# Involution patches by 19 transposes at shifted rows instead of 7 transposes and DMA copies inside SBUF

## The chip, the cores and the metric

The kernel runs on one core of a Trainium2 chip. Its time is the device time of one execution in microseconds (us); the median of the runs is what counts. A profile shows one further execution. All data are f32.

The engines in the profile: PE (matrix products; PEld is its weight load), DVE and ACT (vector and scalar engine), POOL (GpSimd) and SP, which here only issues DMAs. PE's products land in PSUM, eight banks of 512 f32 for each of 128 partitions; the other engines carry them on from there.

## The reference

The input is `x` of 4 images, 256 channels, 56 x 56. Four layers follow each other, each of the form `x = x + layer(group_norm(x))`:

- layer 0, an involution: every pixel has its own 7 x 7 filter for each of 16 groups of 16 channels, made from the pixel's normed channels by two 1x1 convolutions (256 to 64, 64 to 49 x 16).
- layer 1, two 3x3 convolutions with batch norm, relu and a residual.
- layer 2, an involution again, with batch norms and relu.
- layer 3, a gate: the mean real part of a Fourier transform gives one factor per channel.

The involution, cut to what matters:

```python
kern = einsum('bchw,oc->bohw', h, span_w) + span_b        # 49 taps per group and pixel
kern = kern.reshape(b, G, 1, K * K, Ho, Wo)               # G = 16, K = 7
patches = patches.reshape(b, G, c // G, K * K, Ho, Wo)    # the 7x7 surroundings of each pixel
out = (kern * patches).sum(axis=3)
```

## The kernel before

Layers 0 and 2 share one function, `involution_layer`; layer 1 is `conv_layer` between them, and layer 3 is spread over layer 2. The change is in the involution.

An involution layer runs over 8 units: 4 images, 2 blocks `cb` of 128 channels (8 groups of 16). An image of 56 x 56 is cut into 7 columns (`tx`) of 8 pixels, and each column into 19 tiles (`ty`) of 3 x 8 pixels. The surroundings of a tile are 9 x 14 = 126 pixels (`Q`). So the involution of a tile is a matrix product over 126 pixels: a patch `xw` (126 pixels x channels) against a matrix `kt` (126 pixels x 24 outputs) for each group of channels.

A unit has two stages.

The tap stage (`tap_matrices`) makes `kt` of the whole unit: 32 groups of six products of the span table `z_sb` with the bottleneck's output `hp` (L596), each evicted with its bias by DVE (L615) or, every third, by ACT (L608). Callbacks (`hooks`) put other work between the groups.

The apply stage goes over the 7 columns. For each, `apply` multiplies the patches with `kt` (L637). An instruction computes several groups of channels against each other and only the diagonal blocks are wanted. `O_PARTS` (L50) sets two parts: tiles 0 to 9 with four groups at once (64 channels, 96 outputs), in two PSUM banks, and tiles 10 to 18 with two groups at once (32 channels, 48 outputs), in a third bank. ACT scales the first diagonal block into `un` (L650, L652), DVE adds the others (three, then one; L657), and POOL (layer 0, L662) or DVE (layer 2, L664) adds the result to the image.

The patches are made in `next_strip`, `begin_windows` and `next_windows`. `next_strip` norms a column with its borders into the single buffer `strip_sb`, 63 rows of 14 pixels (POOL, L390, or in layer 2 ACT, L388). `begin_windows` transposes 7 pieces of 9 rows on PE (L405): these are the patches of every third tile. `next_windows` copies them from PSUM into `xw` by ACT (L417). The other twelve patches are the same pixels three and six rows further down: four DMAs copy them inside SBUF from partition to partition (L423, L425), on SP's queue, in layer 0 one of them on POOL's. Three buffers `xw` (`NXW`) let the patches be made three columns ahead.

The main loop (L1026 to L1131) gives the order, and `in_order` holds every engine to the order of the program. After a unit's tap stage come the transposes for a column ahead (L1066), and after each column's `apply` the rest of `next_windows`, `next_strip` and the column's statistics (L1115). In layer 0, DVE and PE also prepare the next image (`sums`, `bottleneck`, whose products are L468 and whose evictions are L485 and L487). In layer 2, POOL gates the image before in chunks.

In layer 0, `z_sb` holds the table of all 16 groups. In layer 2 it holds 8, and `load_taps` (L581) loads the next unit's half from `z2_dram` during the apply stage (L1103). `tables2` writes `z2_dram` in layer 0's last units.

PSUM is handed out in pairs of banks (`two_banks`), four pairs in turn.

Of the kernel before, what the change touches and what calls it, by code (L numbers as in the profile page):

```python
# [10 lines left out]
F32 = mybir.dt.float32  # L11
# [38 lines left out]
O_PARTS = ((4, (0, 5), 5, 30), (2, (10,), 9, 26))  # L50
NXW = 3
# [20 lines left out]
def net_kernel(  # L72
# [45 lines left out]
    z2_dram = dram.tile([NB, P, GB, ZN], F32, name="z2_dram")  # L118
# [40 lines left out]
    def batch_norms():  # L159

        folds = (
            ("1", by_channel, L1_G1, L1_B1, L1_M1, L1_V1, NB),
            ("2", by_channel, L1_G2, L1_B2, L1_M2, L1_V2, NB),
            ("4", by_channel, L2_G, L2_B, L2_M, L2_V, NB),
            ("3", by_row, L2_G1, L2_B1, L2_M1, L2_V1, 1),
        )
        for name, par, _, _, _, var, n in folds:
            bn["s" + name] = const.tile([P, n], F32, name=f"bn{name}_s")
            bn["t" + name] = const.tile([P, n], F32, name=f"bn{name}_t")
            rsqrt_eps(bn["s" + name], par(var), BN_EPS)  # L170
        yield

        par_of = bn["par"] = {}
        for n in (2, 4):
            par_of[n] = const.tile([P, n], F32, name=f"par{n}_sb")
            nc.vector.tensor_reduce(
                par_of[n],
                ident_sb.rearrange("p (a e i) -> p e a i", e=n, i=GC),
                mybir.AxisListType.XY,
                ALU.add,  # L180
            )
            yield
        for i in range(3):
            for name, par, gamma, beta, mean, _, _ in folds:
                s, t = bn["s" + name], bn["t" + name]
                if i == 0:
                    nc.vector.tensor_mul(s, s, par(gamma))
                elif i == 1:
                    nc.vector.tensor_mul(t, par(mean), s)
                else:  # L190
                    nc.vector.tensor_sub(t, par(beta), t)
            yield

        s4 = bn["s4"]
        bn["s4"] = {}
        for n in (2, 4):
            bn["s4"][n] = const.tile([P, n, NB], F32, name=f"s4_{n}")
            for i in range(n):
                nc.vector.tensor_scalar_mul(bn["s4"][n][:, i, :], s4, par_of[n][:, i : i + 1])
            yield  # L200
# [98 lines left out]
    def involution_layer(layer, xin, xout, red, span, sb, xs_of, ahead=None, pending=None):  # L299

        with ExitStack() as es:
# [29 lines left out]
            z_sb = wpool.tile([P, G if layer == 0 else GB, ZN], F32, name="z_sb")  # L331
# [35 lines left out]
            strip_sb = wpool.tile([P, HS, QX], F32, name="strip_sb")  # L367
            if layer == 2:
                nc.gpsimd.memset(strip_sb, 0.0)

            def next_strip():
# [5 lines left out]
                st = strip_sb  # L377
# [14 lines left out]
            def window(ty):  # L392

                k, j = divmod(ty, TY)
                return (0, NSB, 2 * NSB - 1)[j] + k

            begun_windows = []

            def begin_windows():

                flat = strips[len(xws)].rearrange("p h w -> p (h w)")
                ps = two_banks().rearrange("p i n -> p (i n)")
                begun_windows.append(ps)
                for k in range(NSB):
                    nc.tensor.transpose(ps[:Q, k * P : (k + 1) * P], flat[:, k * Q : (k + 1) * Q], ident_sb)  # L405

            def next_windows():

                if len(xws) == len(columns):
                    return  # L410
                if not begun_windows:
                    begin_windows()
                ps = begun_windows.pop()
                xw = work.tile([Q, NTY, P], F32, name="xw", bufs=NXW)
                xws.append(xw)

                nc.scalar.copy(xw[:, :NSB, :], ps[:Q, : NSB * P].rearrange("q (n c) -> q n c", n=NSB))  # L417

                n = NSB - 1
                for j in range(1, TY):  # L420
                    cut = TY * QX * j
                    at = window(j)
                    nc.sync.dma_start(xw[: Q - cut, at : at + n, :], xw[cut:Q, 0:n, :])  # L423
                    eng = nc.sync if layer == 2 or j == 1 else nc.gpsimd
                    eng.dma_start(xw[Q - cut : Q, at : at + n, :], xw[:cut, 1 : 1 + n, :])  # L425

# [68 lines left out]
            def begin():  # L495
# [10 lines left out]
                nc.gpsimd.memset(strip_sb, 0.0)  # L506
# [74 lines left out]
            def load_taps(cb):  # L581

                nc.sync.dma_start(z_sb, z2_dram[cb])

            def tap_matrices(b, cb, hooks):
# [3 lines left out]
                for n in range(GB * TP // PB):  # L589
                    g, pb = divmod(n, TP // PB)  # L590
                    ps = two_banks()
                    for k in range(PR):
                        for i in range(2):
# [4 lines left out]
                                z_sb[i * R : (i + 1) * R, cb * GB + g if layer == 0 else g, z0 : z0 + Q],  # L598
# [26 lines left out]
            def apply(b, cb, kt, tx, xw):  # L625

                img = xs_of[b, cb].rearrange("p (h w) -> p h w", w=W)
                y0 = 0
                for ng, tys, nty, rows in O_PARTS:
                    pair = two_banks()  # L630
                    nb, m = len(tys), ng * GC
                    v = pair[:, :nb, : ng * nty * TP].rearrange("p i (e n) -> p i e n", e=ng)
                    for i in range(nb):
                        for k in range(nty):
                            ty = tys[i] + k
                            for j in range(P // m):
                                nc.tensor.matmul(  # L637
                                    v[m * j : m * j + m, i, :, k * TP : (k + 1) * TP],
                                    xw[:, window(ty), m * j : m * j + m],
                                    kt[:, ng * j : ng * j + ng, :, ty * NTX + tx, :],  # L640
                                    start=True,
                                    stop=True,
                                )
                    n = rows // nb * TX
                    o = [v[:, :, e, :n] for e in range(ng)]
                    un = work.tile([P, 2, O_PARTS[0][3] // 2 * TX], F32, name="un")
                    un = un.rearrange("p i n -> p (i n)")[:, : rows * TX]
                    part = un.rearrange("p (i n) -> p i n", i=nb)
                    if layer == 0:
                        nc.scalar.mul(part, o[0], bn["par"][ng][:, 0:1])  # L650
                    else:
                        nc.scalar.activation(  # L652
                            part, o[0], AF.Identity, bias=bn["t4"][:, cb : cb + 1], scale=bn["s4"][ng][:, 0, cb : cb + 1]
                        )
                    for e in range(1, ng):
                        s = bn["par"][ng][:, e : e + 1] if layer == 0 else bn["s4"][ng][:, e, cb : cb + 1]
                        nc.vector.scalar_tensor_tensor(part, o[e], s, part, ALU.mult, ALU.add)  # L657
                    dst = img[:, y0 : y0 + rows, tx * TX : (tx + 1) * TX]
                    y0 += rows
                    u = un.rearrange("p (r x) -> p r x", x=TX)  # L660
                    if layer == 0:
                        nc.gpsimd.tensor_tensor(dst, u, dst, ALU.add)  # L662
                    else:
                        nc.vector.scalar_tensor_tensor(dst, u, 0.0, dst, ALU.max, ALU.add)  # L664
# [166 lines left out]
            def last_normed(b, cb):  # L831
# [6 lines left out]
                else:  # L838
                    z = z_sb.rearrange("p g z -> p (g z)")
                    pieces = [z[:, k * n : (k + 1) * n] for k in range(2)]  # L840
                    pieces += [strip_sb.rearrange("p h w -> p (h w)")[:, :n], dead(b, cb, n, n)]
# [129 lines left out]
            else:  # L971
                since = mark()
                load_taps(0)
                nc.sync.dma_start(zb_sb, zb2_dram)
                next_strip()
                run(bottleneck(0))
                hooks0[3] = list(pending[0])
                for _ in range(NXW - 1):
                    next_windows()
                    next_strip()  # L980
                hooks0[7] = [next_windows, next_strip]
            if layer == 0:
                next_strip()
                for i in range(NXW):
                    hooks0.setdefault(2 + 5 * i, []).extend((next_windows, next_strip))
# [20 lines left out]
            def tables2():  # L1006
# [10 lines left out]
                for i in range(2):  # L1017
                    by = z2[i * R : (i + 1) * R].rearrange("r (cb g) z -> r cb g z", cb=NB)
                    for h in range(2):
                        to = z2_dram[:, h * R : (h + 1) * R].rearrange("cb r (g i) z -> r cb g i z", i=2)  # L1020
                        for c in range(NB):
                            nc.sync.dma_start(to[:, c, :, i], by[:, c])
# [3 lines left out]
            for u, (b, cb) in enumerate(units):  # L1026
# [39 lines left out]
                begin_windows()  # L1066
# [35 lines left out]
                if layer == 2 and u + 1 < len(units):  # L1102
                    late[1].append(lambda cb=cb: load_taps(1 - cb))  # L1103
# [13 lines left out]
                for tx in range(NTX):  # L1117
# [5 lines left out]
                    next_windows()  # L1123
                    next_strip()
# [644 lines left out]
```

## Time and profile before

| | us |
|---|---|
| runs (3), median | 1796.66 |
| runs, lowest to highest | 1794.62 to 1802.1 |
| the profiled execution | 1791.96 |
| its span, first to last instruction | 1790.2 |

The granted clock of PE was 0.983 on average. In that execution layer 0 runs to about 506 us, layer 1 to about 1238, and layer 2 to the end.

How to read the lines below. A line of groups has the source line, engine, operation, what is written and read, the shape (partitions x elements; for PE rows*columns of the weights first), the count, the busy time in us and the mean ns of one, and then the idle time of the engine just before and what ended it. "issue" is idle time in which the engine waited for nothing that the profile shows. PE's times overlap: matmuls are pipelined, and those in different parts of the array run at the same time, so a mean of 207 ns does not mean one in 207 ns. An f32 product is two matmul instructions, each with a weight load; an f32 transpose is one. Queue q8 brings PE's instructions.

### The profile page before, as it was taken

Reading aid. Unit: us, or ns where it says so; the run is one execution under the profiler, and the core shown is the slowest. Engines: PE = TensorE matmul, PEld = TensorE weight load, DVE = VectorE, ACT = ScalarE, POOL = GpSimd, SP = SyncE. Lnnn points to the kernel's source line nnn. Section 1 sums busy time; section 2 is a strip of 40 time slices with the busy share of each in tenths; the row PEclk is TensorE's granted clock in tenths of the full one; section 3 lists DMA queues with packets and bytes.
Section 4 is the critical chain, followed back from the end, with each engine's and each line's share of the span. In section 5 each row is a group of like instructions: output and inputs, shape, how many; then the busy total and the mean of one; then the engine's idle time right before and its main releaser. Section 6 shows DMA issues by size and latency. Waiting matters only on the chain.

```text
span 1790.2 us, 55795 instructions
## 1 busy us (share of the span) xinstructions
PE 1682.8 (94%) x24040; PEld 1469.8 (82%) x24040; DVE 1387.3 (77%) x2745; ACT 822.8 (46%) x1882; POOL 406.8 (23%) x627
## 2 busy tenths in 40 slices
PE   6999999999989999999999999999999899799887
PEld 4887888878878988898889888986887787688775
DVE  2777787776779988998899888985777687677675
ACT  2655556555642313231323122113768577577564
POOL 2224432344310000000000000001000464563572
PEclk9999999999989999999999999999999999999997
DMA  2445444644752112120112011122446667766753
GB/s 86 128 158 172 148 145 134 188 121 130 222 158 91 55 52 64 64 68 29 64 64 70 26 64 37 44 111 74 153 147 186 186 219 210 215 213 178 203 145 119
DMA packets 69043, 221.04 MB, mean 123 GB/s; under 512 B 13461, under 2 KB 23198, under 8 KB 65086
## 3 DMA queue, kind: packets, MB, share of 16 engines
q1 hardware_dynamic: 52302, 150.65, 27.1%
q0 software_dynamic: 14656, 64.77, 11.4%
q8 instruction: 190, 3.11, 0.7%
q10 hardware_dynamic: 1840, 2.05, 0.4%
q14 instruction: 55, 0.45, 0.1%
HBM read 80.91 MB, written 49.81 MB: 73 GB/s over the span
## 4 chain that ended last, share of the span: by engine, by line
PE 64%; DVE 20%; ACT 5%; issue 4%; DMA 4%; POOL 2%; SPq 1%; POOLq 0%; ACTq 0%; DVEq 0%
PE mm L1533 18%; PE ps L596 15%; PE ps L637 9%; PE mm L1451 9%; DVE kt L615 5%; PE mm L1422 5%; DVE un L657 4%; DMA xw<-xw 3%; PE ps L405 2%; PE ps L468 1%; ACT kt L608 1%; DVE st L1115 1%; DVE res L1526 1%; POOL strip_sb L390 1%; DVE xs L1385 1%
## 5 line engine op out<-in xcount | busy, mean ns | idle before, releaser
L596 PE MATMUL ps<-hp,z_sb 64*126 64x133 f32 x6144 | 387.6, 280 | 8.4 <-DVE kt L615 4.2
L637 PE MATMUL ps<-kt,xw 126*32 126x48 f32 (+1 forms) x12544 | 340.4, 223 | 53.3 <-issue 37.5
L596 PEld LDWEIGHTS ps<-hp,z_sb 64*126 64x126 f32 x6144 | 364.7, 186 | 27.7 <-DVE kt L615 6.2
L1533 PE MATMUL mm<-v,u_sb 128*128 128x280 f32 (+1 forms) x1728 | 383.5, 383 | 1.9 <-DVE u_sb L1264 1.5
L637 PEld LDWEIGHTS ps<-kt,xw 126*32 126x32 f32 (+1 forms) x12544 | 302.7, 118 | 99.4 <-issue 71.2
L615 DVE TENSOR_TENSOR kt<-ps,zb_sb 126x798 f32<-126x798 f32 x352 | 332.8, 980 | 63.8 <-PE ps L596 63.2
L1533 PEld LDWEIGHTS mm<-v,u_sb 128*128 128x128 f32 x1728 | 326.1, 189 | 56.3 <-DVE u_sb L1264 1.9
L608 ACT ACTIVATE kt<-ps,zb_sb 126x133 f32<-126x133 f32 x960 | 290.1, 492 | 101.0 <-PE ps L596 101.0
L1451 PE MATMUL mm<-v,u_sb 128*128 128x252 f32 (+1 forms) x936 | 209.7, 384 | 0.0
L1451 PEld LDWEIGHTS mm<-v,u_sb 128*128 128x128 f32 x936 | 176.5, 190 | 30.6 <-issue 0.8
L657 DVE SCALAR_TENSOR_TENSOR un<-ps,s,un 128x240 f32<-128x240 f32 x224 | 102.5, 458 | 90.6 <-ACT un L652 86.2
L1570 POOL DMA_DIRECT2D x<-xs x24 | 13.2, 549 | 680.1 <-DVE xs L1569 426.5
L657 DVE SCALAR_TENSOR_TENSOR un<-ps,par_sb,un 128x240 f32<-128x240 f32 x224 | 98.2, 456 | 77.7 <-ACT un L650 73.4
L1518 ACT ACTIVATE res<-xs,shift,norm_sb 128x1120 f32<-128x1120 f32 (+1 forms) x24 | 30.2, 1258 | 238.5 <-DVE xs L1569 107.3
L405 PE MATMUL ps<-ident_sb,strip_sb 128*126 128x128 f32 x784 | 113.2, 286 | 16.4 <-POOL strip_sb L390 10.5
L417 ACT COPY xw<-ps 126x896 f32<-126x896 f32 x112 | 101.4, 907 | 51.8 <-PE ps L405 43.3
L662 POOL TENSOR_TENSOR xs<-un,xs 128x240 f32<-128x240 f32 x112 | 72.3, 665 | 180.7 <-DVE un L657 180.5
L405 PEld LDWEIGHTS ps<-ident_sb,strip_sb 128*126 128x126 f32 x784 | 86.0, 143 | 28.0 <-POOL strip_sb L390 17.9
L652 ACT ACTIVATE un<-ps,bn_t,s 128x240 f32<-128x240 f32 x112 | 59.6, 538 | 101.4 <-PE ps L637 97.3
L1422 PE MATMUL mm<-xs,u_sb 128*128 128x126 f32 (+1 forms) x792 | 98.7, 277 | 2.1 <-DVE xs L1385 1.0
L650 ACT ACTIVATE un<-ps,par_sb 128x240 f32<-128x240 f32 x112 | 50.0, 448 | 104.0 <-PE ps L637 92.1
L1422 PEld LDWEIGHTS mm<-xs,u_sb 128*128 128x128 f32 x792 | 94.4, 191 | 3.5 <-DVE xs L1438 1.6
(256 smaller groups left out, 1905.8 us busy)
## 6 DMA issues: line engine op xcount, KB each, us to landing
xw<-xw SPq DMA_DIRECT2D x168, 252.0 KB
xw<-xw SPq DMA_DIRECT2D x224, 126.0 KB
xw<-xw POOLq DMA_DIRECT2D x56, 252.0 KB, 4.6
xs<-x SPq DMA_DIRECT2D x24, 560.0 KB
x<-xs POOLq DMA_DIRECT2D x8, 1568.0 KB
xs<-x SPq DMA_DIRECT2D x8, 1568.0 KB
xs<-in_x_dram SPq DMA_DIRECT2D x6, 1568.0 KB
x<-xs SPq DMA_DIRECT2D x6, 1568.0 KB
```

The lines of the kernel that those rows point to most:

```text
L405: nc.tensor.transpose(ps[:Q, k * P : (k + 1) * P], flat[:, k * Q : (k + 1) * Q], ident_sb)
L417: nc.scalar.copy(xw[:, :NSB, :], ps[:Q, : NSB * P].rearrange("q (n c) -> q n c", n=NSB))
L596: nc.tensor.matmul(ps[:Q, i, k * NT : (k + 1) * NT], z_sb[i * R : (i + 1) * R, cb * GB + g if layer == 0 else g, z0 : z0 + Q], hp[i * R : ...
L608: nc.scalar.activation(kt[:, g, pb, :, p], ps[:Q, i, k * NT : (k + 1) * NT], AF.Identity, bias=zb[:, p : p + 1],)
L615: nc.vector.tensor_tensor(kt[:, g, pb].rearrange("q t (i k) -> q t i k", i=2), ps[:Q, :, : PR * NT].rearrange("q i (k t) -> q t i k", k=PR ...
L637: nc.tensor.matmul(v[m * j : m * j + m, i, :, k * TP : (k + 1) * TP], xw[:, window(ty), m * j : m * j + m], kt[:, ng * j : ng * j + ng, :, ...
L652: nc.scalar.activation(part, o[0], AF.Identity, bias=bn["t4"][:, cb : cb + 1], scale=bn["s4"][ng][:, 0, cb : cb + 1])
L657: nc.vector.scalar_tensor_tensor(part, o[e], s, part, ALU.mult, ALU.add)
L662: nc.gpsimd.tensor_tensor(dst, u, dst, ALU.add)
L1422: nc.tensor.matmul(ps[:, co * m : (co + 1) * m], u[ci][:, co * P : (co + 1) * P], v2[:, e, : n // 2, ci * WT : (ci + 1) * WT], start=(ci = ...
L1451: nc.tensor.matmul(ps, u1_sb[:, ci, dy, k, co * P : (co + 1) * P], v[:, k, dy * NB + ci : (dy + n - 1) * NB + ci + 1 : NB, :], start=(j == 0),
L1533: nc.tensor.matmul(ps, u2_sb[:, ci, dy, k, co * P : (co + 1) * P], v[:, k, dy * NB + ci : (dy + n - 1) * NB + ci + 1 : NB, :], start=(j == 0),
```

## The change

The twelve patches that were copied are now transposed as well, each from its own rows of the strip: 19 transposes per column, in three groups of 7, 6 and 6. Each group has a pair of banks, and is copied to `xw` by ACT, ACT and DVE. No DMA copies remain.

All products are of two groups of channels (32 channels, 48 outputs). A column's 19 tiles lie in two banks of ten (tile 9 is computed in both), so that ACT scales, DVE combines and POOL or DVE adds once per column, 448 elements each.

There are two strips instead of one, two `xw` instead of three, one `un` instead of two. The patches are made one column less far ahead: `next_windows` is called whole, once after the tap stage and after each column but the last. The span table `z_sb` is kept whole in layer 2 too: one load at its start in place of one per unit.

```diff
-O_PARTS = ((4, (0, 5), 5, 30), (2, (10,), 9, 26))
-NXW = 3
+NG, NTB = 2, 10
+ROWS_B = H // 2
...
-            strip_sb = wpool.tile([P, HS, QX], F32, name="strip_sb")
+            strip_sbs = [wpool.tile([P, HS, QX], F32, name=f"strip_sb{i}") for i in range(2)]
...
-                xw = work.tile([Q, NTY, P], F32, name="xw", bufs=NXW)
+                flat = strips[len(xws)].rearrange("p h w -> p (h w)")
+                xw = work.tile([Q, NTY, P], F32, name="xw")
                 xws.append(xw)
-
-                nc.scalar.copy(xw[:, :NSB, :], ps[:Q, : NSB * P].rearrange("q (n c) -> q n c", n=NSB))
-
-                n = NSB - 1
-                for j in range(1, TY):
-                    cut = TY * QX * j
-                    at = window(j)
-                    nc.sync.dma_start(xw[: Q - cut, at : at + n, :], xw[cut:Q, 0:n, :])
-                    eng = nc.sync if layer == 2 or j == 1 else nc.gpsimd
-                    eng.dma_start(xw[Q - cut : Q, at : at + n, :], xw[:cut, 1 : 1 + n, :])
-
+                t0 = 0
+                for n, copy in ((7, nc.scalar.copy), (6, nc.scalar.copy), (6, nc.vector.tensor_copy)):
+                    ps = two_banks().rearrange("p i n -> p (i n)")
+                    for k in range(n):
+                        at = (t0 + k) * TY * QX
+                        nc.tensor.transpose(ps[:Q, k * P : (k + 1) * P], flat[:, at : at + Q], ident_sb)
+                    copy(xw[:, t0 : t0 + n, :], ps[:Q, : n * P].rearrange("q (n c) -> q n c", n=n))
+                    t0 += n
...
+                pair = two_banks()
+                v = pair[:, :, : NG * NTB * TP].rearrange("p i (e n) -> p i e n", e=NG)
+                m = NG * GC
+                for i in range(2):
+                    for k in range(NTB):
+                        ty = i * (NTB - 1) + k
+                        for j in range(P // m):
+                            nc.tensor.matmul(
+                                v[m * j : m * j + m, i, :, k * TP : (k + 1) * TP],
+                                xw[:, ty, m * j : m * j + m],
+                                kt[:, NG * j : NG * j + NG, :, ty * NTX + tx, :],
+                                start=True,
+                                stop=True,
+                            )
+                row = pair[:, 0, : ROWS_B * TX]
+                o = [
+                    bass.AP(row.tensor, row.offset + e * NTB * TP, [row.ap[0], [512 + TX, 2], [1, ROWS_B * TX]])
+                    for e in range(NG)
+                ]
+                un = work.tile([P, H * TX], F32, name="un", bufs=1)
...
-                begin_windows()
+                next_windows()
+                next_strip()
...
-                if layer == 2 and u + 1 < len(units):
-                    late[1].append(lambda cb=cb: load_taps(1 - cb))
...
                     apply(b, cb, kt, tx, xws[u * NTX + tx])
-                    next_windows()
-                    next_strip()
+                    if tx < NTX - 1:
+                        next_windows()
+                        next_strip()
```

## The prediction, made before the result

> **What bounds the kernel now.** I read the page first: who is busy, and which queues move what.
>
> ```profile
> PE 1682.8 (94%) x24040; PEld 1469.8 (82%) x24040; DVE 1387.3 (77%) x2745; ACT 822.8 (46%) x1882; POOL 406.8 (23%) x627
> ...
> q1 hardware_dynamic: 52302, 150.65, 27.1%
> q0 software_dynamic: 14656, 64.77, 11.4%
> q8 instruction: 190, 3.11, 0.7%
> ```
>
> PE sets the end, and the chain that ended last agrees (PE 64%, DVE 20%). So whatever PE is given or spared counts. Note the last line: PE's 24040 weight loads and 24040 matmuls arrive as 190 packets of 16 KB, one packet for some 126 pairs of a weight load and a matmul.
>
> The change lies in the "apply" stages: 7 columns of a unit, 16 units. Next, their groups with shapes kept apart:
>
> ```profile
> L637 PE MATMUL ps<-kt,xw 126*64 126x96 f32 x4480 | 228.9, 251 | 16.7 <-DMA xw<-xw 10.6 <-DVE un L657 3.5 <-issue 1.1
> L637 PE MATMUL ps<-kt,xw 126*32 126x48 f32 x8064 | 120.8, 207 | 36.6 <-issue 36.4
> L405 PE MATMUL ps<-ident_sb,strip_sb 128*126 128x128 f32 x784 | 113.2, 286 | 16.4 <-POOL strip_sb L390 10.5 <-issue 2.4 <-ACT hp L487 1.6
> L417 ACT COPY xw<-ps 126x896 f32<-126x896 f32 x112 | 101.4, 907 | 51.8 <-PE ps L405 43.3 <-DMA xw<-xw 8.1
> L657 DVE SCALAR_TENSOR_TENSOR un<-ps,s,un 128x240 f32<-128x240 f32 x168 | 78.5, 467 | 79.5 <-ACT un L652 75.2
> ```
>
> Divided by 112 columns: 40 matmul instructions of the 64-channel form, 72 of the 32-channel form (an f32 product is two), 7 transposes. The DMA copies that the change removes cost PE 10.6 us in all; "issue" cost it 36.4, nearly all in the 32-channel form. What "issue" is, the timeline of PE's weight loads shows (start, length, group, and in brackets the idle time before it):
>
> ```profile
> 321.83 2.39 PEld L637 LDWEIGHTS ps<-kt,xw 126*64 126x64 f32 x81 [0.17 <-issue]
> 325.00 0.41 PEld L637 LDWEIGHTS ps<-kt,xw 126*32 126x32 f32 x31 [0.78 <-issue]
> 325.47 0.75 PEld L405 LDWEIGHTS ps<-ident_sb,strip_sb 128*126 128x126 f32 x7
> 326.39 2.47 PEld L637 LDWEIGHTS ps<-kt,xw 126*64 126x64 f32 x88 [0.17 <-issue]
> 329.49 0.33 PEld L637 LDWEIGHTS ps<-kt,xw 126*32 126x32 f32 x24 [0.63 <-issue]
> 329.88 0.75 PEld L405 LDWEIGHTS ps<-ident_sb,strip_sb 128*126 128x126 f32 x7
> 330.80 2.53 PEld L637 LDWEIGHTS ps<-kt,xw 126*64 126x64 f32 x95 [0.17 <-issue]
> 334.19 0.27 PEld L637 LDWEIGHTS ps<-kt,xw 126*32 126x32 f32 x17 [0.86 <-issue]
> ```
>
> Between two stalls lie 31+7+88 = 126 and 24+7+95 = 126 pairs: exactly one packet of q8. PE runs out of instructions at the packet's edge, and 4.49 and 4.70 us pass from one resumption to the next, where the pairs alone stream in 3.7. In the trace's packet times a stalled PE resumes 1.2 to 1.65 us after the end of the newest q8 packet, and the next one starts only after PE has entered the block before it: one block is fetched ahead, no more. Call the time from entering a block to having the next one F.
>
> Last, three apply stages as windows (length, then busy time of each engine, clock, DMA share, GB/s):
>
> ```profile
> 190.50:217.20 26.70, 24.75 (x819) 21.97 (x819) 17.09 (x39) 11.18 (x19) 16.33 (x24) 1.00 0.53 152
> 245.20:279.60 34.40, 31.20 (x856) 25.30 (x855) 23.50 (x56) 17.48 (x39) 17.29 (x26) 1.00 0.47 131
> 1529.60:1565.10 35.50, 26.35 (x820) 22.71 (x819) 21.16 (x49) 17.66 (x25) 23.18 (x33) 1.00 0.81 223
> ```
>
> PE is busy through layer 0's stages (the second one also holds the next image's 56 long L468 matmuls); layer 2's wait more, under a DMA share of 0.8. In these three no other engine is over 70% busy.
>
> **The change, part by part.** Per column, on PE:
>
> Products: 112 instructions become 160 (2 x 10 x 4 products), all 32-channel. In unstalled runs 40 of the 64-channel form take 1.80 us to the next group and 72 of the other 0.91 (starts 11.0 ns apart). After: 160 x 11.0 ns + 0.13 = 1.89 us, where 2.71 was spent: -0.8.
>
> Transposes: 7 become 19. Seven take 0.91 us (0.109 to 0.118 apart, and the switch); 19 take 2.2 to 2.4: +1.4. A column then streams in 4.2 us instead of 3.6.
>
> Seven columns do not pay all of it. Of the groups of a unit, one stands between the tap products and the first column, where PE waits some 1.5 us for DVE's last two kt copies (980 ns each) anyway, and none any longer between the last column and the next unit's tap products. So 7 x 1.89 + 6 x 2.4 = 27.6, about 28 us of streaming.
>
> Waits that go: L405's waits for the strip (28.4 us in all over 51 times; two strips now) and the DMA waits. What is late next is the instruction stream: a column is 179 pairs instead of 119. A unit's stage is 7 x 160 + 6 x 19 = 1234 pairs or 9.8 blocks, of which half a block is in hand at the start: 9.3 to fetch.
>
> F has three parts: from entering a block to the packet's start, the packet (1.11 us on average over q8), and 1.4 to resume. The first part was 2.0 to 2.9 us in stalls at DMA shares of 0.5 to 0.8, but 0.6 to 1.2 where the queues were idle. The copies that go are 168 x 252 + 224 x 126 + 56 x 252 KB = 85 of 221 MB, almost all of the traffic in layer 0's stages and over half in layer 2's. No row has this stream without them, so F is bounded by 2.7 (0.6+0.9+1.2) below and the present 4.5 above. I take 3.4 (0.95+1.1+1.4), and 3.7 in layer 2 where the gate of the image before runs.
>
> Of five consecutive blocks three hold a whole group of transposes and 107 products (2.2 + 1.3 = 3.5 us) and two products alone (1.4), which wait for F. A stage takes 9.3 x (0.6 x max(F, 3.5) + 0.4 x F): 32.2 us at 3.4, 34.4 at 3.7; add 0.15 to the next tap product.
>
> Before (first L637 to the next L596, from the timeline) against after, units 0 to 7 being layer 0:
> - Units 0, 2, 4, 6: 29.2, 28.0, 29.8, 28.2 against 32.3 each: +14.0.
> - Units 1, 3, 5 with the L468 matmuls: 35.3, 35.4, 36.1. These cost 6.6 us now (34.3 against 27.7); under them some 0.9 of fetch hides, so 32.3 + 5.7 = 38.0: +7.2.
> - Unit 7, with five groups: 29.7 against 31.6: +1.9.
> - Unit 8: 30.6 against 32.3: +1.7. Units 10, 12, 14: 33.4, 36.5, 38.1 against 34.5 each: -4.5.
> - Unit 9: 33.1 against 38.0: +4.9. Units 11, 13: 35.9, 35.4 against 40.2 each: +9.1.
> - Unit 15: 32.6 against 33.8: +1.2.
>
> Sum: +35.5 us.
>
> The rest lies under this. ACT per column: copies 0.91 and about 0.8, one 448-element scaling 0.73 (from 552 and 524 ns for 240 and 208), in layer 2 a strip of 1.05: 3.5 of 4.6 us. With six L487 pieces of 0.49 it is 6.4 in four columns of units 9, 11, 13, at most 3 us more in each; none taken, since today's 5.9 there costs little. DVE: four operations of 467 and 428 ns become one of 0.72, and a 768-element copy of some 0.9 comes in (798 elements take L615 0.98): 1.83 against 1.6 us. The copy waits for the third group of transposes with bn_stats and the next column's combination behind it on DVE; PE needs that combination's banks only after 19 more transposes, 2.3 us on. POOL: 0.70 + 0.63 becomes 1.15, its DMA issue (565 ns) goes. One `un` buffer: scaling, combination and add take 2.6 of a column's 4.6 us. SP loses 0.78 us of issue per copy and seven z loads; the one load at layer 2's start doubles, and has from 1241.2 to 1250.2 while PE waits for ACT's L487. The second strip's memset (0.8 us of POOL) has the same cover; without covers the two would cost about 4 us. All these at nothing.
>
> So 1792.0 + 35.5 = 1827.5 in the profiled execution's terms; the median of the runs is 4.7 above that execution: 1832.
>
> **A rule against this row.** The Trainium skill's page "Runtime: NRT & Kernel Launch", section "Instruction fetch mechanics", has the same blocks of 256 instructions, but calls the cost of crossing one mostly hidden, since issuing is slower than filling. The trace shows the blocks and not the hiding (0.63 to 0.86 us at each edge above). By the rule no stage would stall, which is the far end of the first rival below: 1753.
>
> **The rivals.**
>
> Fetch keeps up. With the queues empty F drops under 2.75, and streaming alone decides: 28 to 30 us a stage where 26.7 to 36 stand now. For it: units 1 to 3 show hardly a stall even at a DMA share of 0.5. Against it: there 119 pairs lasted 3.9 us, so that a block had over 4 us. The sum falls by 6 us for each 0.1 us of F under 3.5, is zero at F = 2.9, and with no stall at all (28.2 us a stage, 34 with L468) it is -44: 1753 to 1787.
>
> F does not fall. Image loads, gates and q8's own latency keep it at 4.0 (4.4 beside gates): 37.2 and 40.9 us a stage, +120: 1917. For it: with a share of 0.8, single blocks took 5 to 9 us in units 11 to 15. Against it: most of that share goes.
>
> A new wait between engines (three of four bank pairs per column are transposes', two patch buffers instead of three): 0.3 us per column would add 34: 1866. For it: layer 0 loses that much now to the single strip. Against it: each pair is reused a full column later.
>
> The change not doing what it says: the patches are recomputed exactly, one tile row twice; no rival.
>
> **How the numbers follow.** This kernel's runs differ by about 0.4%, so 0.5% (9 us) is what can be told from no change. Chances: forecast, F from 3.1 to 3.7: 0.55; fetch keeps up: 0.17; F stays at 4: 0.08; a new wait: 0.10; near zero, F 2.8 to 3.0: 0.10. Range: from F = 2.85 (-3: 1793) to F = 3.7, 4.0 beside gates (34.4 and 37.2 us a stage: +75, 1872), with a little of the new wait (1878). Faster 0.17; same 0.13; slower 0.70.
>
> **What would show it.** About 242 packets of q8 (52 more). L637's idle on "issue" grows from 108.6 us to some 180, at every 126th pair inside runs of 160. Layer 0's column period 4.5 to 4.8 us; starts of products 11 ns apart, transposes 0.11 to 0.12. DMA share in layer 0's stages under 0.15. No waits for DMA xw, hardly one for strips. If stages of layer 0 end within 30 us, F is wrong; if PE waits on ACT or DVE rather than "issue", the new wait is it.

## The result, and the profile after

The changed kernel takes 1890.64 us (median of 4 runs, 1885.07 to 1895.76) against 1799.38 us for the kernel before (4 runs, 1794.62 to 1802.77): a ratio of 1.0509 [1.0466, 1.0551], slower by 91 us. The forecast was 1832 with a range to 1878: the sign and the main mechanism are right; the size is far too small, and two places that cost time, the gaps and the taps below, were put at nothing. The profiled execution took 1895.76 us, its span 1894.0 us against 1790.2 before, the mean granted clock 0.974 against 0.983.

From the page's parts 1 and 3, the engines (busy time, share, instructions) and the queues (packets, MB, share of 16 engines' span):

```profile
PE 1744.7 (92%) x30760; PEld 1542.6 (81%) x30760; DVE 1355.8 (72%) x2460; ACT 872.0 (46%) x1882; POOL 374.0 (20%) x517
...
q1 hardware_dynamic: 22222, 74.42, 11.7%
q0 software_dynamic: 11072, 50.32, 7.5%
q8 instruction: 241, 3.95, 0.9%
```

What the edit promised is there: the copies are gone from q1 and q0 (131 MB in all instead of 221), and DVE and POOL have less to do. What it costs is there too: 6720 more matmuls and as many more weight loads on PE, and 241 packets of instructions instead of 190. PE's busy time rose by 62 us, the span by 104: most of the rest is waiting. Part 5 says for what (busy time, mean ns of one, then the idle time before them by releaser; L613 are the products, L405 the transposes, L574 the tap products, L593 DVE's kt copies):

```profile
L574 PE MATMUL ps<-hp,z_sb 64*126 64x133 f32 x6144 | 388.8, 279 | 16.4 <-DVE kt L593 12.3
L613 PE MATMUL ps<-kt,xw 126*32 126x48 f32 x17920 | 237.1, 207 | 81.6 <-issue 81.0
L613 PEld LDWEIGHTS ps<-kt,xw 126*32 126x32 f32 x17920 | 212.9, 110 | 116.0 <-issue 103.7
L405 PE MATMUL ps<-ident_sb,strip_sb 128*126 128x128 f32 x2128 | 276.7, 287 | 21.7 <-issue 17.9
```

The products' matmuls wait for nothing but "issue", 81.0 us in 52 waits, and their weight loads have 103.7 us of it: no DMA, no strip. The 10.4 us that the profile puts down to ACT or DVE before these weight loads are twelve gaps of 0.80 us behind the next image's long matmuls, while PE is busy, and five of 0.17 us. The strip (L391) holds the transposes' matmuls once, for 0.3 us.

The timeline of PE's weight loads in unit 2 of layer 0 (start, length, group, idle time before it) shows the waits:

```profile
199.82 0.54 PEld L574 LDWEIGHTS ps<-hp,z_sb 64*126 64x126 f32 x8
200.48 2.06 PEld L405 LDWEIGHTS ps<-ident_sb,strip_sb 128*126 128x126 f32 x19
202.71 1.79 PEld L613 LDWEIGHTS ps<-kt,xw 126*32 126x32 f32 x160 [0.17 <-issue]
204.57 2.06 PEld L405 LDWEIGHTS ps<-ident_sb,strip_sb 128*126 128x126 f32 x19
206.79 1.61 PEld L613 LDWEIGHTS ps<-kt,xw 126*32 126x32 f32 x142 [0.17 <-issue]
210.23 0.31 PEld L613 LDWEIGHTS ps<-kt,xw 126*32 126x32 f32 x18 [1.83 <-issue]
210.61 2.06 PEld L405 LDWEIGHTS ps<-ident_sb,strip_sb 128*126 128x126 f32 x19
212.83 1.08 PEld L613 LDWEIGHTS ps<-kt,xw 126*32 126x32 f32 x91 [0.17 <-issue]
214.33 0.84 PEld L613 LDWEIGHTS ps<-kt,xw 126*32 126x32 f32 x69 [0.42 <-issue]
215.24 2.06 PEld L405 LDWEIGHTS ps<-ident_sb,strip_sb 128*126 128x126 f32 x19
217.47 0.50 PEld L613 LDWEIGHTS ps<-kt,xw 126*32 126x32 f32 x39 [0.17 <-issue]
218.16 1.39 PEld L613 LDWEIGHTS ps<-kt,xw 126*32 126x32 f32 x121 [0.19 <-issue]
```

The first column, which still has instructions in hand, takes 4.08 us (202.71 to 206.79): 1.86 for 160 products and 2.22 for 19 transposes. Then PE halts 18+19+91 = 128 and 69+19+39 = 127 pairs apart, that is once per packet of q8, and 4.10 and 3.83 us pass from one resumption to the next (210.23, 214.33, 218.16). These pairs alone would stream in some 2.7 us. The queues had nearly nothing else to carry, as the windows show (length, busy time of PE, PEld, DVE, ACT, POOL, clock, DMA share, GB/s); the first is this stage, the second unit 4's, the third unit 10's in layer 2:

```profile
202.70:236.30 33.60, 27.74 (x1235) 25.51 (x1234) 16.91 (x26) 13.93 (x19) 13.59 (x13) 1.00 0.02 4
333.30:370.40 37.10, 30.54 (x1235) 28.28 (x1234) 16.90 (x26) 14.05 (x19) 13.59 (x13) 0.91 0.02 4
1474.00:1513.70 39.70, 29.81 (x1235) 27.10 (x1234) 19.41 (x26) 21.12 (x26) 24.76 (x34) 0.96 0.28 85
```

Units 2 and 4 hold the same work at the same DMA share of 0.02, yet unit 4 is 3.5 us longer and its clock is 0.91. From its timeline of weight loads:

```profile
337.34 1.61 PEld L613 LDWEIGHTS ps<-kt,xw 126*32 126x32 f32 x138 [0.17 <-issue]
341.17 0.51 PEld L613 LDWEIGHTS ps<-kt,xw 126*32 126x32 f32 x22 [2.23 <-issue]
341.80 3.35 PEld L405 LDWEIGHTS ps<-ident_sb,strip_sb 128*126 128x126 f32 x19
```

And the five microseconds around the wait as a window:

```profile
340.00:345.00 5.00, 3.83 (x39) 3.71 (x40) 0.68 (x1) 1.77 (x3) 1.14 (x1) 0.66 0.02 3
```

After a wait of 2.23 us the granted clock is half for 3.41 us, and 19 transposes take 3.35 us instead of 2.06. So part of the wait for instructions is paid a second time, in clock.

Where the 104 us of the span went, worked out from PE's matmul records over the 16 units ("taps" from a unit's first to its last tap product, "gap" from there to the first product of its first column, "stage" from there to the next unit's first tap product):

| us | before | after | difference |
|---|---|---|---|
| stages | 527.1 | 597.6 | +70.5 |
| gaps | 18.3 | 39.3 | +21.0 |
| taps | 422.6 | 432.0 | +9.4 |
| all else (start, the work between the layers, end) | 822.2 | 825.1 | +2.9 |

The forecast had +35.5 in the stages and nothing elsewhere. The gap of the kernel before, in its unit 2, shows what ends it (start, length, group, idle time before it; the last tap product starts at 189.41):

```profile
189.95 0.98 DVE L615 TENSOR_TENSOR kt<-ps,zb_sb 126x798 f32<-126x798 f32 x1
...
190.52 0.19 PEld L637 LDWEIGHTS ps<-kt,xw 126*64 126x64 f32 x2 [0.17 <-issue]
...
190.98 3.37 PEld L637 LDWEIGHTS ps<-kt,xw 126*64 126x64 f32 x123 [0.27 <-DVE kt L615]
```

Seven transposes fill the gap to 190.52; then PE starts its products, and waits for DVE's last kt copy until 190.98, 1.57 us after the last tap product. In the changed kernel, nineteen transposes fill 2.43 us.

### The profile page after: what moved, and what is told of

Its sections match the earlier page's. It is cut to its first block, busy times and chain, and to the rows that moved or that the text cites. A ratio compares the mean times of both kernels' runs of the same rounds, so it can differ in the third digit from the quotient of the medians.

```text
span 1894.0 us, 67604 instructions
## 1 busy us (share of the span) xinstructions
PE 1744.7 (92%) x30760; PEld 1542.6 (81%) x30760; DVE 1355.8 (72%) x2460; ACT 872.0 (46%) x1882; POOL 374.0 (20%) x517
## 5 line engine op out<-in xcount | busy, mean ns | idle before, releaser
L574 PE MATMUL ps<-hp,z_sb 64*126 64x133 f32 x6144 | 388.8, 279 | 16.4 <-DVE kt L593 12.3
L574 PEld LDWEIGHTS ps<-hp,z_sb 64*126 64x126 f32 x6144 | 364.1, 185 | 36.3 <-DVE kt L593 15.9
L593 DVE TENSOR_TENSOR kt<-ps,zb_sb 126x798 f32<-126x798 f32 x352 | 332.5, 980 | 57.2 <-PE ps L574 56.7
L613 PE MATMUL ps<-kt,xw 126*32 126x48 f32 x17920 | 237.1, 207 | 81.6 <-issue 81.0
L613 PEld LDWEIGHTS ps<-kt,xw 126*32 126x32 f32 x17920 | 212.9, 110 | 116.0 <-issue 103.7
L405 PE MATMUL ps<-ident_sb,strip_sb 128*126 128x128 f32 x2128 | 276.7, 287 | 21.7 <-issue 17.9
L405 PEld LDWEIGHTS ps<-ident_sb,strip_sb 128*126 128x126 f32 x2128 | 245.8, 146 | 32.9 <-issue 20.0
L406 ACT COPY xw<-ps 126x896 f32<-126x896 f32 x224 | 181.4, 857 | 54.8 <-PE ps L405 54.7
L406 DVE COPY xw<-ps 126x768 f32<-126x768 f32 x112 | 107.1, 957 | 90.3 <-PE ps L405 88.6
L634 DVE SCALAR_TENSOR_TENSOR un<-ps,s,un 128x448 f32<-128x448 f32 x56 | 38.3, 684 | 132.8 <-ACT un L630 132.8
L634 DVE SCALAR_TENSOR_TENSOR un<-ps,par_sb,un 128x448 f32<-128x448 f32 x56 | 38.1, 680 | 90.0 <-ACT un L628 90.0
L149 POOL TENSOR_TENSOR norm_sb<-norm_sb,mhalf 128x1 f32<-128x1 f32 x32 | 19.7, 619 | 415.2 <-DVE norm_sb L148 415.1
L638 POOL TENSOR_TENSOR xs<-un,xs 128x448 f32<-128x448 f32 x56 | 63.9, 1142 | 175.2 <-DVE un L634 173.4
```

Of the source, the lines that this page charges most:

```text
L405: nc.tensor.transpose(ps[:Q, k * P : (k + 1) * P], flat[:, at : at + Q], ident_sb)
L406: copy(xw[:, t0 : t0 + n, :], ps[:Q, : n * P].rearrange("q (n c) -> q n c", n=n))
L574: nc.tensor.matmul(ps[:Q, i, k * NT : (k + 1) * NT], z_sb[i * R : (i + 1) * R, cb * GB + g, z0 : z0 + Q], hp[i * R : (i + 1) * R, py, px]. ...
L593: nc.vector.tensor_tensor(kt[:, g, pb].rearrange("q t (i k) -> q t i k", i=2), ps[:Q, :, : PR * NT].rearrange("q i (k t) -> q t i k", k=PR ...
L613: nc.tensor.matmul(v[m * j : m * j + m, i, :, k * TP : (k + 1) * TP], xw[:, ty, m * j : m * j + m], kt[:, NG * j : NG * j + NG, :, ty * NT ...
L634: nc.vector.scalar_tensor_tensor(part, o[1], s, part, ALU.mult, ALU.add)
```

## The experiments

Four stories were in play: PE waits for instruction blocks ("fetch", the forecast's); PE streams longer because of the transposes ("streaming"); the engines wait on one another with three of four bank pairs taken ("engines"); and, for the gaps, whether transposes ahead of the first column are free. The first five runs tell these apart, the last two try to use what they showed.

**1. The products alone.** The kernel before, patches still copied by DMA, with the new 32-channel products and their combination.

```diff
-O_PARTS = ((4, (0, 5), 5, 30), (2, (10,), 9, 26))
+NG, NTB = 2, 10
+ROWS_B = H // 2
...
-                for ng, tys, nty, rows in O_PARTS:
-                    pair = two_banks()
...
-                        for k in range(nty):
-                            ty = tys[i] + k
...
+                pair = two_banks()
...
+                for i in range(2):
+                    for k in range(NTB):
+                        ty = i * (NTB - 1) + k
+                        for j in range(P // m):
+                            nc.tensor.matmul(
+                                v[m * j : m * j + m, i, :, k * TP : (k + 1) * TP],
+                                xw[:, window(ty), m * j : m * j + m],
...
```

> The kernel before with the new products alone: all tiles by 32-channel products, one combination per column; the patches still by 7 transposes and DMA copies. Theory 1, PE waits for its own instructions, one block of 126 pairs at a time, each needing F: a column has 167 pairs instead of 119, a stage 8.8 blocks to fetch, at F = 4.4 us in layer 0 and some 5.5 in layer 2, where the copies load the queues: stages of 39 and 48 us instead of 28 and 35, about +175 us, 1970 (1900 to 2030). Theory 2, PE's streaming work sets the time: a column streams 0.8 us less, -90 us, 1710. Theory 3, waits between engines set it: fewer operations on ACT, DVE and POOL, so 1750 to 1800.

Measured: 1946.69 us, ratio 1.0825 [1.0783, 1.0868], +149 us. A column's stream is shorter than before (1.86 us of products instead of 2.71, the same seven transposes), DVE and ACT have less to do, and yet with run 3 it is the slowest of all. The timeline of its weight loads (same columns; L636 are the products):

```profile
221.68 1.55 PEld L636 LDWEIGHTS ps<-kt,xw 126*32 126x32 f32 x128 [1.37 <-issue]
227.60 0.20 PEld L636 LDWEIGHTS ps<-kt,xw 126*32 126x32 f32 x7 [4.37 <-issue]
227.91 1.35 PEld L406 LDWEIGHTS ps<-ident_sb,strip_sb 128*126 128x126 f32 x7
```

A block of 128 pairs streams in 1.55 us and the next is there 5.9 us after it began. The products' idle time on "issue" is 220.2 us, over 109 times. Streaming and engines are out as what sets this time: of the work of PE, ACT and DVE, only the number of PE's instructions went up. The total lies in theory 1's range, but its split does not hold: stages average 42.1 us in layer 0 and 41.6 in layer 2, where 39 and 48 were expected.

**2. The transposes alone.** The changed kernel with the products of the kernel before (64 and 32 channels, 112 matmuls per column instead of 160).

```diff
-NG, NTB = 2, 10
-ROWS_B = H // 2
+O_PARTS = ((4, (0, 5), 5, 30), (2, (10,), 9, 26))
...
-                for i in range(2):
-                    for k in range(NTB):
-                        ty = i * (NTB - 1) + k
...
+                for ng, tys, nty, rows in O_PARTS:
+                    pair = two_banks()
...
+                                    xw[:, ty, m * j : m * j + m],
...
```

> The changed kernel with the products and combinations of before: 19 transposes per column alone, two strips, two patch buffers, no copies in SBUF. Theory 1 (fetch): 131 pairs per column, 6.6 blocks to fetch in a stage, 24 us at F = 3.7, under the 33 us that PE streams (7 x 2.71 + 6 x 2.3): hardly a stall left, L637 idle on issue under 40 us instead of 185, stages of 33 us (39 with L468), with the late stage starts 1865, about 25 faster than the changed kernel. Theory 2 (streaming): 0.8 us per column more than the changed kernel, 1980. Theory 3 (engines): DVE has 2 operations more per column, so the changed kernel's time or more, 1890 to 1930.

Measured: 1874.68 us, ratio 1.0427 [1.0398, 1.0456], +77 us. The window of the same stage:

```profile
202.70:236.30 33.60, 33.60 (x910) 31.10 (x910) 23.82 (x46) 16.59 (x28) 14.36 (x19) 1.00 0.02 4
```

PE is busy in all of it. The products' "issue" falls to 0.8 us, and stages with six groups of transposes and without the next image's matmuls take 32.7 to 33.8 us, where pure streaming was put at 33. With the strips and the patch buffers of the changed kernel, hardly more than the waits for DVE's combination before the transposes (9.1 us in 18 waits) is new. So the engine story is out: with 131 pairs a column, a block of 126 streams in 4.6 us and the fetch hides under it. The forecast of 1865 was 10 us short; stages with the next image's matmuls took 41.1 to 42.2 us where 39 was expected.

**3. The copies' traffic put back.** The changed kernel with four DMAs per column of the size of the old copies, from the span table to scratch in DRAM that nobody reads.

```diff
+    from_z = z_sb.rearrange("p g z -> p (g z)")
+    for j in range(1, TY):
+        cut = TY * QX * j
+        to = idle[4 * (len(xws) % 2) + 2 * (j - 1) :]
+        nc.sync.dma_start(to[0][: Q - cut], from_z[cut:Q, : 6 * P])
+        nc.sync.dma_start(to[1][Q - cut : Q], from_z[:cut, : 6 * P])
```

> The changed kernel with DMA traffic put back that nothing waits for: four DMAs per column on SP's queue, of the sizes of the old patch copies, from z_sb to unread scratch in DRAM. Theory 1 (fetch): F rises from some 3.7 us to 4.4 in layer 0 and 5.5 in layer 2; 9.3 blocks a stage: +6 and +16 us a stage, about +160 us, 2050 (1970 to 2100). Theories 2 and 3: nothing that PE streams or waits for is touched, 1880 to 1900.

Measured: 1946.14 us, ratio 1.0808 [1.0763, 1.0853], 55 us over the changed kernel. Traffic that nobody waits for does slow PE: "issue" grows (the products' 81.0 becomes 115.6, the transposes' 17.9 becomes 25.1), and the half-rate clock behind such waits with it (some 48 us in the units become 110). But the forecast for it was three times that, and even its range was missed; the split is uneven: layer 2's stages grew from 305.0 to 352.5 us, layer 0's only from 292.6 to 307.1. Two windows, one in each layer:

```profile
202.60:236.60 34.00, 27.19 (x1076) 25.09 (x1075) 15.10 (x24) 13.03 (x19) 11.42 (x11) 0.95 0.25 78
1474.00:1520.00 46.00, 35.46 (x939) 31.16 (x938) 21.89 (x39) 23.48 (x51) 17.80 (x26) 0.93 0.64 204
```

The median time from one stalled resumption to the next, 126 pairs on, was 4.02 us in layer 0 (13 times; 3.83 without the traffic) and 5.66 in layer 2 (24 times; 4.02 without). These DMAs write to DRAM where the old copies stayed in SBUF, and load the queues less in layer 0 (0.25 in this stage, 0.53 in the kernel before), so this is not the price of the old copies.

**4. Half the products.** The changed kernel without the products of the second bank; the second half of a column is combined from the first bank's.

```diff
-                for i in range(2):
+                for i in range(1):
...
-                    bass.AP(row.tensor, row.offset + e * NTB * TP, [row.ap[0], [512 + TX, 2], [1, ROWS_B * TX]])
+                    bass.AP(row.tensor, row.offset + e * NTB * TP, [row.ap[0], [TX, 2], [1, ROWS_B * TX]])
```

> The changed kernel without the products of the second bank (tiles 9 to 18); the second bank's part of each column is combined from the first bank's results. 80 instead of 160 product instructions per column, all else as it was. Theory 1 (fetch): 99 pairs per column, 4.9 blocks a stage, 18 us at F = 3.7, under the 21 us of streaming: stages of 21 to 22 us (27 with L468), about -230 us, 1660 (1630 to 1700). Theory 2 (streaming): 80 x 11 ns = 0.88 us per column, -99 us, 1792. Theory 3 (engines): ACT, DVE and POOL have the same work, so 1850 to 1890.

Measured: 1690.37 us, ratio 0.9404 [0.9375, 0.9433]: 200 us less than the changed kernel. The 80 products taken out of each column stream in 0.88 us, 99 us over 112 columns; the other half of the gain is waits and the half-rate clock behind them (some 48 us become 7). Stages fall to 20.3 us where they hold nothing else, which is their streaming (7 x 0.98 + 6 x 2.22 = 20.2), "issue" to 2.9 us. All transposes, copies, strips and buffers are as in the changed kernel, so none of these was what held its stages.

**5. The first column's transposes moved into the tap stage.** After the tap groups 9, 15 and 21 go 7, 6 and 6 transposes, and ACT copies all three groups.

```diff
+                ahead_of = window_steps((nc.scalar.copy,) * 3)
+                place(hooks, ahead_of, (9, 15, 21))
+                hooks[21].append(next_strip)
                 kt = tap_matrices(b, cb, hooks)
-
-                next_windows()
-                next_strip()
```

> The changed kernel with the 19 transposes that stand between the tap stage and the first column moved into the tap stage (after its groups 9, 15 and 21), copied by ACT. Theory A, these transposes are serial there: from the last tap product to the first product it is 2.43 us instead of 1.57, and the tap stage, which DVE's evictions set, has 4 us of PE to spare: 16 x 0.86 = -14 us, 1877 (1872 to 1882). Theory B, they only fill time in which PE would wait for its next block anyway: no change, 1885 to 1895. Theory C, PE has nothing to spare in the tap stage: it grows by 2 us, up to 1905.

Measured: 1912.48 us, ratio 1.0617 [1.0579, 1.0656], 22 us worse than leaving them. The gaps fell from 39.3 to 3.6 us, but the taps rose from 432.0 to 483.0, 3.2 us a unit for transposes that take 2.2. And the old wait came back (weight loads after the last tap products; L617 are the products):

```profile
204.82 2.01 PEld L578 LDWEIGHTS ps<-hp,z_sb 64*126 64x126 f32 x33
206.96 0.15 PEld L617 LDWEIGHTS ps<-kt,xw 126*32 126x32 f32 x6
208.40 1.79 PEld L617 LDWEIGHTS ps<-kt,xw 126*32 126x32 f32 x154 [1.29 <-ACT kt L590]
```

So PE has no slack inside the tap stage: in the kernel before it was busy for 23.79 of the 24.00 us of unit 2's, and in this run for 27.03 of 27.70, so the growth is PE's own work and no wait for ACT's added copies. The 4 us that theory A gave PE are not there. The result lies outside all three theories; C, which lets the tap stage grow by 2 us, is the nearest. Behind the tap stage there are some 1.4 us in which PE waits for kt whatever it does; the forecast was right that they exist, and wrong that 19 transposes fit in.

**6. The second strip alone.** The kernel before with two strips in layer 0.

```diff
-            strip_sb = wpool.tile([P, HS, QX], F32, name="strip_sb")
+            strip_sbs = [wpool.tile([P, HS, QX], F32, name=f"strip_sb{i}") for i in range(2 if layer == 0 else 1)]
...
-                st = strip_sb
+                st = strip_sbs[len(strips) % len(strip_sbs)]
```

> The kernel before with a second strip buffer in layer 0 alone, where transposes waited 28 us in all for the strip. If streaming sets layer 0's stages without that wait: 25.5 us instead of 28 to 29.7, -20 us, 1778. If fetch does (119 pairs in 3.6 us are faster than F = 4.3 beside the copies' traffic; 6.1 blocks x 4.3): 26.5 us, -10 us, 1788.

Measured: 1799.45 us (12 runs), ratio 1.0005 [0.9981, 1.0028]. No change; both figures, 1778 and 1788, were missed. In layer 0 (45 to 515 us of both profiles) PE's matmuls waited 0.6 us for the strip instead of 10.5. In its place they waited longer for instructions (the products' "issue" 11.5 us instead of 8.1), for the copies (5.0 instead of 1.1) and for DVE's combination (5.6 instead of 2.5, products and L468 together): the waits moved, and the 10.5 us were never a price. The 28 us of the forecast were not 28 us of time either: they add the matmuls' 10.5 us and the weight loads' 17.9, which are largely the same waits counted twice. (Over the whole execution the waits for the copies rose from 10.6 to 21.5 us, but most of that, 9.6 to 16.6, is in layer 2, where this edit changes nothing.)

**7. Thirteen transposes in layer 2.** The same, and in layer 2 the first six copied patches are transposed and copied by DVE; the other six stay with DMA, products as before.

```diff
+                if layer == 2:
+                    ps = two_banks().rearrange("p i n -> p (i n)")
+                    begun.append(ps)
+                    for k in range(NSB - 1):
+                        at = k * Q + TY * QX
+                        nc.tensor.transpose(ps[:Q, k * P : (k + 1) * P], flat[:, at : at + Q], ident_sb)
...
+                for ps in more:
+                    nc.vector.tensor_copy(xw[:, NSB : NSB + n, :], ps[:Q, : n * P].rearrange("q (n c) -> q n c", n=n))
+                for j in range(1 + len(more), TY):
```

> The kernel before with two strips in layer 0 and, in layer 2, 13 transposes per column: the six patches three rows down are transposed and copied by DVE, the six patches six rows down are still copied by DMA. Fetch theory: in layer 2 a stage streams 28.6 us and fetches 6.4 blocks at some 4.4 us (the queues' load halves), 28.3: stages without L468 at 29 to 30 us instead of 30.6 to 38, those with L468 at 36 instead of 35: -18, with the strips 1770 (1760 to 1785). If waits between engines set layer 2's stages, more transposes and copies only add: 1800 to 1810.

Measured: 1807.36 us (12 runs), ratio 1.0042 [1.0024, 1.006], slower by 0.4%. The products' "issue" fell to 13.3 us and the DMA waits to 6.0, so the edit did what it was for. But layer 2's stages hardly moved (276.8 us; 275.5 in the kernel before): those that hold the next image's matmuls rose from 33 to 36 us to 38.6, and the gaps from 1.12 to 1.77 us a unit. What PE did not wait there, it spent on 336 more transposes and in new waits for DVE's combination (before the products 12.2 us instead of 3.5, before L468's matmuls 9.5 instead of 1.8). The fetch theory's 1760 to 1785 was missed, and the time lies in the range of the other story, waits between engines (1800 to 1810). Of the versions that do all the work, none that I found beats the kernel before.

## Why the prediction was wrong in size

Two columns of this table, set against each other, sort the runs: how long 126 pairs stream, and F. Pairs are a weight load and a matmul; "126 pairs stream in" is worked out from the stage's pairs and the unstalled lengths above (1.86 us for 160 products, 2.22 and 0.91 for 19 and 7 transposes, the forecast's 2.71 for the old products; for run 2 its 32.8 us stages), F is the median time between two resumptions after "issue" gaps of over 0.18 us, 120 to 132 pairs apart, among products and transposes (5 and 12 times in the kernel before, 14 and 20 after, 45 and 35 in run 1), half clock the time of half-rate clock records within the units of a layer, without the one that both kernels have at the start of unit 0:

| kernel | pairs per column | 126 pairs stream in | F, layer 0 / 2 | "issue" before products | half clock, layer 0 / 2 | stages | result |
|---|---|---|---|---|---|---|---|
| 4, half the products | 99 | 3.8 us | hardly any | 2.9 | 0 / 6.8 | 389.5 | 0.940 |
| before | 119 | 3.8 | 4.70 / 5.28 | 37.5 | 0 / 17.7 | 527.1 | 1 |
| 2, transposes alone | 131 | 4.6 | hardly any | 0.8 | 0 / 2.8 | 574.8 | 1.043 |
| after | 179 | 2.7 | 3.83 / 4.02 | 81.0 | 22.2 / 25.7 | 597.6 | 1.051 |
| 1, products alone | 167 | 2.1 | 4.56 / 4.84 | 220.2 | 105.9 / 99.5 | 669.3 | 1.083 |

Where a block streams for longer than F, PE streams; where it is shorter, PE waits for F (in the kernel before only in part: few of its blocks lie between two stalls). It also accounts for +149 and +77 making +91 together: the transposes lengthen each block's stream from 2.1 to 2.7 us under the same wait, without the copies F is 3.8 us in layer 0 instead of 4.6, and the half-rate time falls from 205 to 48 us. Added to the new products, the transposes save 57 us; added to the old ones, they cost 77.

The profiled execution took 68 us more than its forecast of 1827.5: 34.8 in the stages, 21.0 in the gaps, 9.4 in the taps and 2.9 elsewhere. Step by step:

- **The column's stream** was put at 4.2 us and took 4.08. Right, and run 2 confirms it with stages of 32.7 us.
- **The number of packets** (242; 241), no DMA waits, one strip wait, the products' idle time on "issue" (some 180 us; 81.0 before matmuls and 103.7 before weight loads, which together are the forecast's count), a DMA share of 0.02: all as announced. The engines' edits were put at nothing, and no wait on ACT, DVE or POOL appeared before the products' matmuls.
- **F at 3.4 and 3.7 us** is the first step that failed: 3.83 and 4.02. Of its three parts it was the first that was taken too small: the next packet started 1.22 us after a resumption in layer 0 and 1.39 in layer 2 (medians; 0.95 taken). The packet took 1.1 us and PE resumed 1.4 us after its end, both as taken. The median of the stalled blocks is not the mean of all: unit 2's 33.7 us for 9.3 blocks ask for 3.6 in the forecast's formula. The two units of layer 0 whose stages ran wholly at full clock, 0 and 2, took 34.1 and 33.7 us against 32.3, 1.8 and 1.4 us more: over eight units some 13, an estimate, of the 17.8 us that layer 0's stages missed. In layer 2 they missed 17.0, of which units 10 and 14 (39.9 against 34.5) hold 10.8; these have single waits of 2.9 and 3.9 us at a share of 0.28, and half-rate clock, while units 11 to 13 came in within 0.4 us of the forecast.
- **The clock was left out.** A stall has a second price: half-rate clock after it. In the units' stages and taps there were 47.9 us of it, 17.7 before. Unit 4's stage, with two such pieces of 3.41 us, took 3.6 us longer than unit 2's with none: about half of the half-rate time is lost, so at most some 15 us for the 30 us that came in. How the 34.8 us that the stages missed divide between F and clock is an estimate; no run took the clock's part away and left the stalls.
- **Transposes ahead of the first column at nothing** is the step that failed outright: +21.0 us of gaps, 2.43 us a unit instead of 1.11. The cover named for them, PE's wait for the last kt copies, was sized rightly: 1.5 us in the forecast, 1.57 from the last tap product to the end of the wait in the kernel before. But the forecast's own 2.2 to 2.4 us for 19 transposes are longer than that cover, and what sticks out was not put into the sum. It measured 0.86 us a unit (2.43 less 1.57), some 14 us in all; the other 7 of the 21.0 are the 0.46 us from the first product to the end of the kt wait, which the stages of the kernel before held. The one other place that was tried for these transposes, run 5, was worse.
- **The closing transposes "go"** and so they did, but in layer 0 the tap stage does not end sooner for it. The last product of unit 2 and the last tap product of unit 3 are 26.9 us apart in both kernels (217.20 to 244.1 before, 236.25 to 263.1 after). What PE gains at the tap stage's start it gives back in longer taps, +9.4 us over all units, most of it in waits for DVE's kt copies (12.3 us instead of 4.2).

Of the rivals, the new wait between engines (1866) and F staying at 4 (1917) lie on either side of the result. The first has no row before the products' matmuls. The second named the right quantity: F fell, from 4.70 to 3.83 and from 5.28 to 4.02, but ended nearer to its 4.0 in layer 0 than to the forecast's 3.4. "Fetch keeps up" failed in every stage. The Trainium skill's page "Runtime: NRT & Kernel Launch", section "Instruction fetch mechanics", calls the crossing of a block mostly hidden. The forecast's estimate by that rule was 1753; here the crossing is hidden in run 2, with 0.8 us of waits, and not in run 1, with 220.2: it depends on how long 126 pairs stream.

## What to carry to other kernels

Count instructions per microsecond as well as streaming: a PE stage has two speeds, its stream and its 126 pairs per F (here 3.8 us with idle queues, 4.6 to 5.7 at DMA shares of some 0.4 to 0.8), and narrower tiles save the first and raise the second. Before an operation is called free under a wait, compare its length with that wait's, 2.43 with 1.57 us here, and ask what is next in line when a wait goes: the strip's 10.5 us came back as waits for instructions, for the copies and for DVE. Two edits that share a bound need not add: the transposes cost 77 us or save 57, depending on what stands beside them.

## What the runs showed of the hardware

Fetch has a price without traffic too. With a DMA share of 0.02 and 4 GB/s, PE still gets its instructions in blocks of 126 pairs 3.5 to 4.1 us apart.

The granted clock goes down after far less idleness than I would have thought. The half-rate pieces lie on a fixed grid of 3.41 us (341.08 and 354.74 are four steps apart). I added up the time between PE's matmul records in each step of that grid within the stages of the changed kernel, leaving out steps that were themselves at half rate: all 14 steps that a half-rate one follows held 1.91 us or more of it, all 134 that a full-rate one follows 1.80 or less. In the other runs the edge is in the same place, but less sharp: no step with over 1.99 us is followed by full rate, and the least before a half-rate one is 1.73. So a stall of some 2 us can cost clock if it falls within one step of the grid, and need cost none if it straddles two: in unit 2 the 2.00 us before 236.00 straddle 235.28 and cost nothing, in unit 4 the 2.04 us before 353.79 do not straddle and the next step is at half. The Trainium skill's page "TensorE: Matmul & The Clock Gate", section "HAM oscillation — how this bites in real kernels", gives the rule as no idle gaps over about 3.4 us; the window's length agrees with this trace, the length of the harmful gap does not. What is counted within a step stays open: by the weight loads' records instead, one step with 2.49 us of gaps, all of it under long matmuls, is followed by full rate.
